# Names moved in an order written out by hand: block 0's row fetch, five pieces of list scatters, two accumulating scatters, one normalisation step

## The chip, the cores and the metric

The kernel runs on one core of a Trainium2 chip. The metric is device time in microseconds of one execution. An engine here is TensorE (PE, with its weight loads as PEld), VectorE (DVE), ScalarE (ACT), GpSimd (POOL) or SyncE (SP), which only issues DMAs. Each engine works through its own instructions in order.

## The reference, cut to what matters

Eight sequences of 512 tokens, 256 wide, go through two layers.

```python
x = x + L0_ffn(L0_cond(x))          # low-rank adapter, then a fake-quantised gated FFN
h = L1_cond(x)                      # per-language adapter, LayerNorm with per-language gamma and beta
probs = softmax(h @ Wr)             # 9 experts, each token goes to its top 2
topk_w, topk_idx = top_k(probs, 2); topk_w = topk_w / sum(topk_w)
x = x + sum over the 2 experts e:  w_e * ((silu(h @ Wg[e]) * (h @ Wu[e])) @ Wd[e])
```

The second layer's experts take 2 x 4096 token rows. Which rows go to which expert is known only on the chip.

## The kernel before, in words

The first part (up to about 85 us) does layer 0 up to its hidden activations. The second part mixes three streams of small steps ("pieces"), each a Python function that issues the instructions of one step for one batch or block:

- for each batch b (0 to 7): the end of layer 0 (qa, qd, dp, dv), the adapter of layer 1 (ap, aa, xp, xa, zp, zv), LayerNorm (np, nv, na, nw), transposes (tp, ta), the router (cp, ce, ct, cv, ca) and ranks (hp, hv);
- hg, for batch b and quarter j: two indirect DMAs on POOL (line 880) that scatter 128 rows of the batch, 1040 bytes each, into the expert lists in DRAM;
- for each block i of 128 list rows (the experts' work): R fetches the rows (four DMAs on line 1057 and a tag on line 1060, issued by SP), U and W fetch the expert's gate/up and down weights (lines 1067 and 1077, 1408 and 768 KB, skipped when the buffer already holds that expert), t transposes the rows on DVE (line 1088), g multiplies by gate and up on TensorE (line 1098), va to vd do SiLU and the product, w the row weights, d multiplies by down (line 1146), y scales the result on DVE (line 1152), and s adds it into the output with an accumulating indirect DMA on POOL (line 1156).

The plan of the first eight blocks is made after two batches, that of the next after six (pp, pw, lines 953 to 1015).

The order of the pieces is the string ORDER (line 58), and `run` (line 1192) issues them one after the other. From it follows each engine's and each queue's order. Nothing is rearranged afterwards, except that waits on semaphores are put in where a piece needs another's result or reuses a buffer. Waits that matter here:

- R reads the lists at places known only on the chip, so it waits for all list scatters that stand before it in ORDER, and a list scatter waits for all R that stand before it;
- s adds into rows known only on the chip, so each s waits for the s before it to have landed, and for the plain writes of the output (xs, line 710) before it;
- y alternates between three buffers (`y_sb[i % 3]`), so y5 waits for s2, y6 for s3, y7 for s4; row and tag buffers go round by eight;
- np, on POOL, computes the power -1/2 of the variance (lines 739 and 740) and needs zv of its batch; nv on DVE needs np.

After block 13 the loop of lines 1230 to 1236 goes on block by block with the same pieces.

Of the kernel before, what the change touches and what calls it, by code (L numbers as in the profile page):

```python
# [55 lines left out]
LAST_LOAD = "L_dT"  # L56
ZEROS_BEHIND = 12
ORDER = """
    qa0d fa1 fa0 fa2 qa0b qd0d qa0a qd0b qa0c fg0 fg1 qd0a qa2b qd0c dp0b qa1b qa1a dp0a qd1b dv0b qd1a dv0a dp1b
    qd2b qa2a xp0_1 dv1b xp0_0 ap0 xa0_1 qd2a xa0_0 dp1a qa2c xs0 aa0 qd2c qa4a zp0_0 dv1a zp0_1 zv0_0 qa3b ap1 fa3  # L60
    zv0_1 qa3a dp2a qd3b np0 aa1 qd3a dp2b dv2a pu1 pd0 nv0 dp3a dv2b na0_1 qd4a pu2 na0_0 nw0_1 xp1_1 ap2 qa4c
    xa1_1 nw0_0 xp1_0 qa4b zp1_1 dv3a xa1_0 tp0_0 pu0 aa2 zv1_1 zp1_0 ta0_0 qd4b tp0_1 qa5b zv1_0 dp3b ta0_1 qd4c
    np1 qa6b cp0 dv3b xs1 dp4b qd5b ce0 qa5a nv1 fa4 ct0 ap3 dv4b na1_1 mz0 cv0 dp4a na1_0 qa6c pd2 xp2_0 aa3 pd1
    xp2_1 nw1_1 hp0 ca0 fg2 xa2_1 hv0 tp1_1 xa2_0 zp2_1 ta1_1 xs2 nw1_0 hg0_0 zp2_0 zv2_1 tp1_0 fa5 ta1_0 zv2_0
    hg0_2 cp1 qd5a ce1 dv4a ct1 fg3 cv1 dp5b hg0_1 ap4 qd6b ca1 hp1 dv5b np2 aa4 dp5a hv1 qa6a hg0_3 nv2 pp0a qa7a
    pw0a dv5a pp0b pw0b na2_1 ap5 hg1_1 qd6a na2_0 pp0c qd6c nw2_1 dp6b qa7b hg1_3 nw2_0 xp3_1 xp3_0 xa3_1 pw0c fg4
    tp2_0 xa3_0 zp3_1 ta2_0 hg1_2 dv6b xs3 tp2_1 zv3_1 zp3_0 ta2_1 U0 qd7b cp2 aa5 zv3_0 hg1_0 ce2 fa6 dp6a qd7a
    ct2 dp7a dv6a np3 cv2 U1 dp7b W1 ap6 nv3 ca2 R0 dv7b na3_1 hp2 dv7a na3_0 xp4_0 hv2 xa4_0 xp4_1 nw3_0 R1 zp4_0
    xa4_1 zp4_1 nw3_1 tp3_0 aa6 t0 tp3_1 ta3_0 zv4_1 g0a W0 ta3_1 xs4 w0 zv4_0 fa7 cp3 va0 t1 hg2_1 g0b ce3 w1 fg5
    ct3 g0c vb0 np4 cv3 U2 g1a vc0 hg2_0 W2 nv4 g1b ca3 U3 vd0 va1 na4_1 hg2_2 g1c vb1 na4_0 nw4_1 d0 vc1 U4 hg2_3  # L70
    nw4_0 vd1 tp4_1 y0 xp5_0 ta4_1 s0 xp5_1 xa5_0 tp4_0 xa5_1 fg6 zp5_0 ta4_0 zp5_1 zv5_0 W3 cp4 zv5_1 ap7 ce4 R2
    ct4 np5 hp3 aa7 cv4 xs5 hv3 ca4 R3 nv5 hp4 hv4 na5_0 na5_1 t2 xp6_1 R4 w2 g2a xa6_1 nw5_0 nw5_1 tp5_0 va2 zp6_1
    ta5_0 t3 R5 d1 w3 zv6_1 t4 w4 tp5_1 y1 R6 xp6_0 ta5_1 s1 g2b xa6_0 zp6_0 vb2 W4 cp5 zv6_0 R7 g2c ce5 np6 g3a t5
    vc2 w5 nv6 vd2 ct5 xs6 na6_0 g3b U5 cv5 na6_1 d2 va3 fg7 hg3_3 nw6_1 ca5 nw6_0 hp5 W5 hg3_1 tp6_1 g3c hv5 ta6_1
    y2 tp6_0 vc3 U6 t6 xp7_0 hg4_0 ta6_0 w6 xp7_1 vb3 xa7_0 xa7_1 vd3 zp7_0 pp1a hg5_3 zv7_0 cp6 g4a ce6 pw1a xs7
    hg4_1 pp1b va4 g4b pw1b pp1c vb4 hg3_0 g4c pw1c d3 t7 vc4 U7 w7 hg3_2 vd4 g5a y3 W6 s2 d4 va5 hg4_3 g5b y4 W7
    s3 g5c vb5 hg4_2 g6a vc5 U8 vd5 hg5_2 g6b va6 g6c vb6 hg5_0 d5 vc6 U9 vd6 hg5_1 zp7_1 y5 ct6 W8 g7a zv7_1 s4
    cv6 d6 np7 va7 R8 nv7 ca6 na7_0 g7b s5 y6 na7_1 nw7_0 R9 hp6 g7c hv6 tp7_0 nw7_1 vc7 s6 ta7_0 R10 t8 tp7_1 w8
    g8a vb7 ta7_1 vd7 t9 d7 va8 w9 U10 R11 g8b y7 t10 s7 w10 cp7 vb8 g8c ce7 R12 ct7 g9a vc8 cv7 g9b va9 W10 t11
    ca7 U11 vd8 g9c w11 vb9 hg6_2 W9 d8 t12 vc9 w12 vd9 U12 hg6_1 g10a y8 W11 g10b s8 va10 hg6_3 g10c vb10 d9 vc10  # L80
    U13 vd10 hg6_0 g11a y9 W12 s9 d10 va11 R13 g11b y10 s10 g11c vb11 R14 g12a vc11 vd11 t13 d11 va12 w13 U14 R15
    g12b t14 y11 s11 g12c vb12 W14 hp7 vc12 R16 g13a hv7 vd12 pp2a va13 g13b pw2a R17 pp2b vb13 d12 pw2b W13 pp2c
    y12 U15 g13c pw2c s12 W15 vc13 hg7_3 U16 vd13 hg7_0 hg7_1 hg7_2
"""
BLOCKS_IN_ORDER = 14

# [1234 lines left out]
```

## Time and profile before

| | us |
|---|---|
| median of 9 runs | 727.85 |
| lowest, highest | 725.87, 733.16 |
| the profiled execution | 733.25 |
| its span on the core | 731.5 |
| TensorE busy in the span | 676.3 (92%) |
| DVE, ACT, POOL busy | 338.4, 202.1, 206.7 |

In the profile's timelines a line gives the start in the span, the duration, the engine, the line of the kernel, what is written and read and how many instructions are merged; in brackets stand the idle time before it and what ended it. SPq is the queue of SP's DMA issues. In the page's slices each digit is the busy share of a fortieth of the span in tenths.

### The profile page before, as it was taken

How to read it: one execution, taken by the hardware profiler on the slowest of the kernel's cores; microseconds unless marked ns; L12 is line 12 of the kernel's file. 1: busy time of each engine (PE TensorE's matmuls, PEld its weight loads, DVE VectorE, ACT ScalarE, POOL GpSimd, SP SyncE). 2: the span in 40 equal slices, each digit the busy share in tenths (PEclk: the TensorE clock that was granted, in tenths of full speed). 3: DMA queues.
4: the chain of work that ended last, by engine and by line, in shares of the span. 5: the costliest groups of instructions: out<-in, count | busy, mean ns of one | idle time of the engine just before them, and what ended most of it. 6: DMA issues, size and time to landing. Idle time of an engine off the chain costs nothing. (4 is left out here: it accounts for less than half of the span.)

```text
span 731.5 us, 14632 instructions
## 1 busy us (share of the span) xinstructions
PE 676.3 (92%) x4678; PEld 569.8 (78%) x4688; DVE 338.4 (46%) x1036; ACT 202.1 (28%) x407; POOL 206.7 (28%) x190
## 2 busy tenths in 40 slices
PE   9989798678786899999999999999999999999995
PEld 3333254337685789898999999999999999999994
DVE  3989778555763164343333333333333333333331
ACT  4698686432422031111111111111111111111110
POOL 1046304605155524343112121212112112211212
PEclk9999898789897989999999999999999999999998
DMA  9500049357467968333356533279924488235742
GB/s 356 196 4 1 1 166 360 119 164 229 84 184 233 307 175 230 60 67 55 56 135 198 160 46 51 45 224 337 290 31 117 101 286 256 32 43 152 231 89 32
DMA packets 86641, 107.91 MB, mean 148 GB/s; under 512 B 58904, under 2 KB 75424, under 8 KB 82976
## 3 DMA queue, kind: packets, MB, share of 16 engines
q1 hardware_dynamic: 73696, 89.61, 39.7%
q0 software_dynamic: 12720, 17.31, 12.4%
q8 instruction: 39, 0.64, 0.3%
q14 instruction: 42, 0.34, 0.2%
q10 hardware_dynamic: 144, 0.01, 0.0%
HBM read 183.55 MB, written 22.83 MB: 282 GB/s over the span
## 5 line engine op out<-in xcount | busy, mean ns | idle before, releaser
L1098 PE MATMUL bank<-upper__104,lower 128*128 128x128 f32 x2636 | 315.8, 278 | 9.6 <-issue 6.4
L1098 PEld LDWEIGHTS bank<-upper__104,lower 128*128 128x128 f32 x2636 | 311.5, 195 | 15.4 <-issue 8.8
L1156 POOL DMA_INDIRECT out_dram<-upper__104,tag x67 | 103.9, 1551 | 370.1 <-DVE upper__104 L1088 277.4
L1114 DVE TENSOR_TENSOR upper__104<-bank,upper__104 128x512 f32<-128x512 f32 x67 | 46.3, 692 | 173.0 <-PE bank L1098 150.1
L1108 ACT ACTIVATE upper__104<-bank 128x512 f32<-128x512 f32 x67 | 40.0, 597 | 245.6 <-PE bank L1098 190.0
L880 POOL DMA_INDIRECT lists<-row,sloti x64 | 63.5, 992 | 49.4 <-issue 18.2
L1146 PE MATMUL bank<-upper__104 128*128 128x256 f32 x312 | 73.5, 386 | 0.0
L1146 PEld LDWEIGHTS bank<-upper__104 128*128 128x128 f32 x312 | 58.8, 195 | 7.3
L1146 PE MATMUL tok<-upper__104 128*128 128x256 f32 x216 | 49.6, 379 | 0.0
L1146 PEld LDWEIGHTS tok<-upper__104 128*128 128x128 f32 x216 | 39.7, 190 | 4.6
L1146 PE MATMUL bank<-lower,upper__104 128*128 128x256 f32 x180 | 41.9, 380 | 1.2 <-issue 1.2
L1124 ACT ACTIVATE upper__104<-bank 128x128 f32<-128x128 f32 x41 | 11.4, 278 | 112.6 <-PE bank L1098 99.5
L1152 DVE TENSOR_SCALAR upper__104<-bank,wt 128x256 f32<-128x256 f32 x41 | 19.8, 484 | 46.7 <-PE bank L1146 42.7
L1098 PE MATMUL tok<-upper__104,lower 128*128 128x128 f32 x312 | 39.1, 275 | 0.0
L1146 PEld LDWEIGHTS bank<-lower,upper__104 128*128 128x128 f32 x180 | 33.0, 190 | 5.9 <-issue 1.9
L1098 PEld LDWEIGHTS tok<-upper__104,lower 128*128 128x128 f32 x312 | 36.9, 192 | 0.0
L1130 DVE TENSOR_TENSOR upper__104<-bank,upper__104 128x128 f32<-128x128 f32 x41 | 11.9, 290 | 41.0 <-ACT upper__104 L1125 34.2
L718 PE MATMUL tok<-w,ha 65*128 65x256 f32 x64 | 19.2, 439 | 12.4 <-ACT xtok L706 8.3
L506 ACT ACTIVATE g<-wide,swg 128x1024 f32<-128x1024 f32 (+1 forms) x24 | 24.1, 1041 | 3.1 <-PE wide L482 2.5
L1124 ACT ACTIVATE upper__104<-tok 128x128 f32<-128x128 f32 x26 | 7.2, 278 | 64.1 <-PE tok L1098 64.1
L718 PEld LDWEIGHTS tok<-w,ha 65*128 65x128 f32 x64 | 12.8, 216 | 15.2 <-ACT xtok L706 8.8
L640 PE MATMUL bank<-yq,wdT 128*128 128x512 bf16 x75 | 21.6, 412 | 1.0 <-DVE yq L628 0.5
(215 smaller groups left out, 699.7 us busy)
## 6 DMA issues: line engine op xcount, KB each, us to landing
lower<-in_L_ffn_W_dram SPq DMA_DIRECT2D x73, 1408.0 KB
upper__104<-in_L_ffn_W_dram SPq DMA_DIRECT2D x48, 768.0 KB
lower<-in_L_ffn_W_dram SPq DMA_DIRECT2D x24, 768.0 KB
lower<-lists SPq DMA_DIRECT2D x144, 32.0 KB
upper__104<-lists SPq DMA_DIRECT2D x140, 32.0 KB
x_sb<-in_x_dram SPq DMA_DIRECT2D x8, 512.0 KB
out_dram<-xtok SPq DMA_DIRECT2D x8, 512.0 KB
lists<-pad SPq DMA_DIRECT2D x10, 130.0 KB
```

The costliest lines, as they stand in the source:

```text
L506: nc.scalar.activation(g, pg, AF.Silu, scale=swg[:, m : m + 1])
L640: nc.tensor.matmul(pd, lhsT=wdT[:, m, cs], rhs=hq_sb[b % 2][:, m], start=m == 0, stop=False)
L718: nc.tensor.matmul(pz[:, j * D : (j + 1) * D], lhsT=ha_sb[b % 2][:, at : at + P], rhs=batches[b]["w2"], start=False, stop=True, skip_group ...
L880: nc.gpsimd.indirect_dma_start(out=own_rows[(b * NJ + j) * 2 + n], out_offset=bass.IndirectOffsetOnAxis(ap=sloti_sb[b % 3][:, j, n : n + 1 ...
L1098: nc.tensor.matmul(pg[:, at * P : (at + 1) * P], lhsT=gu_sb[i % NW][:, c, n * P : (n + 1) * P], rhs=xbT_sb[i % 3][:, c], start=c == 0, sto ...
L1108: nc.scalar.activation(g_sb[i % 3][:, :4].rearrange("p m t -> p (m t)"), held.pop(("pg", i, "a")), AF.Silu)
L1114: nc.vector.tensor_tensor(hid_sb[i % 3][:, :4].rearrange("p m t -> p (m t)"), held.pop(("pg", i, "b")), g_sb[i % 3][:, :4].rearrange("p m ...
L1124: nc.scalar.activation(gs[:, 4], pg[:, :P], AF.Silu)
L1130: nc.vector.tensor_tensor(hid[:, 4], pg[:, P : 2 * P], gs[:, 4], ALU.mult)
L1146: nc.tensor.matmul(po[:, :D], lhsT=hid_sb[i % 3][:, m], rhs=dn_sb[i % NW][:, m], start=m == 0, stop=m == NM - 1)
L1152: nc.vector.tensor_scalar(y_sb[i % 3], held.pop(("po", i))[:, :D], small_["wt"][i % NX], None, ALU.mult)
L1156: nc.gpsimd.indirect_dma_start(out=out, out_offset=bass.IndirectOffsetOnAxis(ap=tag_sb[i % NX][:, 0:1].bitcast(I32), axis=0), in_=y_sb[i % 3],
```

## The change

Only the string ORDER changes; the same 588 names are in it, and it is wrapped at another width, so that all later line numbers are lower by one. In place of the diff, whose every line is rewrapped, here are the moves:

```diff
- cv2 U1 dp7b W1 ap6 nv3 ca2 R0 dv7b
+ cv2 R0 U1 dp7b W1 ap6 nv3 ca2 dv7b

- g5a y3 W6 s2 d4 va5 hg4_3 g5b y4 W7 s3 g5c vb5 hg4_2 g6a vc5 U8 vd5 hg5_2 g6b va6 g6c vb6 hg5_0 d5 vc6 U9 vd6
- hg5_1 zp7_1 y5 ct6 W8 g7a zv7_1 s4 cv6 d6 np7 va7 R8
+ g5a y3 W6 hg4_3 hg4_2 hg5_2 hg5_0 hg5_1 d4 va5 g5b y4 W7 g5c vb5 g6a vc5 U8 vd5 g6b va6 g6c vb6 d5 vc6 U9 vd6
+ zp7_1 s2 y5 ct6 W8 g7a zv7_1 np7 s3 s4 cv6 d6 va7 R8
```

The orders of TensorE, DVE and ACT stay as they were. On SP the five DMAs of R0 now stand ahead of the two of U1 and W1. On POOL five hg (ten list scatters) stand ahead of s2, and np7 ahead of s3 and s4. R0 still stands behind every list scatter of batches 0 and 1. y5 still waits for s2 and y6 for s3; the tag fetches of R10 and R11 now also wait for s2 and s3.

More of the change, by code (lines that the diff above doesn't have):

```diff
@@ L58 @@
 ORDER = """
[L59 to L83, printed above, removed]
+    qa0d fa1 fa0 fa2 qa0b qd0d qa0a qd0b qa0c fg0 fg1 qd0a qa2b qd0c dp0b qa1b qa1a dp0a qd1b dv0b qd1a dv0a dp1b qd2b
@@ new lines @@
+    qa2a xp0_1 dv1b xp0_0 ap0 xa0_1 qd2a xa0_0 dp1a qa2c xs0 aa0 qd2c qa4a zp0_0 dv1a zp0_1 zv0_0 qa3b ap1 fa3 zv0_1
+    qa3a dp2a qd3b np0 aa1 qd3a dp2b dv2a pu1 pd0 nv0 dp3a dv2b na0_1 qd4a pu2 na0_0 nw0_1 xp1_1 ap2 qa4c xa1_1 nw0_0
+    xp1_0 qa4b zp1_1 dv3a xa1_0 tp0_0 pu0 aa2 zv1_1 zp1_0 ta0_0 qd4b tp0_1 qa5b zv1_0 dp3b ta0_1 qd4c np1 qa6b cp0 dv3b
+    xs1 dp4b qd5b ce0 qa5a nv1 fa4 ct0 ap3 dv4b na1_1 mz0 cv0 dp4a na1_0 qa6c pd2 xp2_0 aa3 pd1 xp2_1 nw1_1 hp0 ca0 fg2
+    xa2_1 hv0 tp1_1 xa2_0 zp2_1 ta1_1 xs2 nw1_0 hg0_0 zp2_0 zv2_1 tp1_0 fa5 ta1_0 zv2_0 hg0_2 cp1 qd5a ce1 dv4a ct1 fg3
@@ new lines @@
+    cv1 dp5b hg0_1 ap4 qd6b ca1 hp1 dv5b np2 aa4 dp5a hv1 qa6a hg0_3 nv2 pp0a qa7a pw0a dv5a pp0b pw0b na2_1 ap5 hg1_1
+    qd6a na2_0 pp0c qd6c nw2_1 dp6b qa7b hg1_3 nw2_0 xp3_1 xp3_0 xa3_1 pw0c fg4 tp2_0 xa3_0 zp3_1 ta2_0 hg1_2 dv6b xs3
+    tp2_1 zv3_1 zp3_0 ta2_1 U0 qd7b cp2 aa5 zv3_0 hg1_0 ce2 fa6 dp6a qd7a ct2 dp7a dv6a np3 cv2 R0 U1 dp7b W1 ap6 nv3
+    ca2 dv7b na3_1 hp2 dv7a na3_0 xp4_0 hv2 xa4_0 xp4_1 nw3_0 R1 zp4_0 xa4_1 zp4_1 nw3_1 tp3_0 aa6 t0 tp3_1 ta3_0 zv4_1
+    g0a W0 ta3_1 xs4 w0 zv4_0 fa7 cp3 va0 t1 hg2_1 g0b ce3 w1 fg5 ct3 g0c vb0 np4 cv3 U2 g1a vc0 hg2_0 W2 nv4 g1b ca3
@@ new lines @@
+    U3 vd0 va1 na4_1 hg2_2 g1c vb1 na4_0 nw4_1 d0 vc1 U4 hg2_3 nw4_0 vd1 tp4_1 y0 xp5_0 ta4_1 s0 xp5_1 xa5_0 tp4_0
+    xa5_1 fg6 zp5_0 ta4_0 zp5_1 zv5_0 W3 cp4 zv5_1 ap7 ce4 R2 ct4 np5 hp3 aa7 cv4 xs5 hv3 ca4 R3 nv5 hp4 hv4 na5_0
+    na5_1 t2 xp6_1 R4 w2 g2a xa6_1 nw5_0 nw5_1 tp5_0 va2 zp6_1 ta5_0 t3 R5 d1 w3 zv6_1 t4 w4 tp5_1 y1 R6 xp6_0 ta5_1 s1
+    g2b xa6_0 zp6_0 vb2 W4 cp5 zv6_0 R7 g2c ce5 np6 g3a t5 vc2 w5 nv6 vd2 ct5 xs6 na6_0 g3b U5 cv5 na6_1 d2 va3 fg7
+    hg3_3 nw6_1 ca5 nw6_0 hp5 W5 hg3_1 tp6_1 g3c hv5 ta6_1 y2 tp6_0 vc3 U6 t6 xp7_0 hg4_0 ta6_0 w6 xp7_1 vb3 xa7_0
@@ new lines @@
+    xa7_1 vd3 zp7_0 pp1a hg5_3 zv7_0 cp6 g4a ce6 pw1a xs7 hg4_1 pp1b va4 g4b pw1b pp1c vb4 hg3_0 g4c pw1c d3 t7 vc4 U7
+    w7 hg3_2 vd4 g5a y3 W6 hg4_3 hg4_2 hg5_2 hg5_0 hg5_1 d4 va5 g5b y4 W7 g5c vb5 g6a vc5 U8 vd5 g6b va6 g6c vb6 d5 vc6
+    U9 vd6 zp7_1 s2 y5 ct6 W8 g7a zv7_1 np7 s3 s4 cv6 d6 va7 R8 nv7 ca6 na7_0 g7b s5 y6 na7_1 nw7_0 R9 hp6 g7c hv6
+    tp7_0 nw7_1 vc7 s6 ta7_0 R10 t8 tp7_1 w8 g8a vb7 ta7_1 vd7 t9 d7 va8 w9 U10 R11 g8b y7 t10 s7 w10 cp7 vb8 g8c ce7
+    R12 ct7 g9a vc8 cv7 g9b va9 W10 t11 ca7 U11 vd8 g9c w11 vb9 hg6_2 W9 d8 t12 vc9 w12 vd9 U12 hg6_1 g10a y8 W11 g10b
@@ L84 @@
+    s8 va10 hg6_3 g10c vb10 d9 vc10 U13 vd10 hg6_0 g11a y9 W12 s9 d10 va11 R13 g11b y10 s10 g11c vb11 R14 g12a vc11
+    vd11 t13 d11 va12 w13 U14 R15 g12b t14 y11 s11 g12c vb12 W14 hp7 vc12 R16 g13a hv7 vd12 pp2a va13 g13b pw2a R17
+    pp2b vb13 d12 pw2b W13 pp2c y12 U15 g13c pw2c s12 W15 vc13 hg7_3 U16 vd13 hg7_0 hg7_1 hg7_2
 """
```

## The prediction

> **What bounds the kernel now.** I read the page's 40 slices first, then the table by stage, then TensorE's timeline with the cause of each idle time, then the timelines of the two queues that the change reorders (SP and POOL) and of DVE beside them. The page:
>
> ```profile
> span 731.5 us, 14632 instructions
> PE 676.3 (92%) x4678; PEld 569.8 (78%) x4688; DVE 338.4 (46%) x1036; ACT 202.1 (28%) x407; POOL 206.7 (28%) x190
> ...
> PE   9989798678786899999999999999999999999995
> ...
> DMA  9500049357467968333356533279924488235742
> ```
>
> One slice is 18.3 us. From slice 17 on (about 300 us) PE stands at 9 to the end: the block loop is bound by TensorE, and whatever TensorE is ahead or behind by at 300 us is kept to the end. So each part is worth what it moves in TensorE's arrival there. Both places that the change touches, 150 to 165 us and 230 to 275 us, lie in front of that, where TensorE still waits.
>
> First place: TensorE's, DVE's and SP's timelines, and the table by 2 us, whose last three columns are granted clock, DMA share and GB/s.
>
> ```profile
> 160.35 0.66 PE L776 MATMUL bank<-ident,row 128*128 128x128 f32 x4 [0.63 <-DVE row L768]
> 164.07 3.52 PE L1098 MATMUL bank<-upper__104,lower 128*128 128x128 f32 x16 [3.07 <-DVE upper__104 L1088]
> ...
> 163.71 0.50 DVE L1088 STREAM_TRANSPOSE upper__104<-lower 128x128 f32<-128x128 f32 x2 [3.42 <-DMA lower<-lists]
> ...
> 153.76 0.37 SPq L1067 DMA_DIRECT2D lower<-in_L_ffn_W_dram  x1
> 154.47 0.34 SPq L1077 DMA_DIRECT2D upper__104<-in_L_ffn_W_dram  x1
> 155.89 1.93 SPq L1057 DMA_DIRECT2D lower<-lists  x4
> ...
> 158.00:160.00 2.00, 1.71 (x10) 1.15 (x9) 1.93 (x4) 1.22 (x4) 0.00 (x0) 1.00 0.93 385
> 162.00:164.00 2.00, 0.00 (x0) 0.00 (x0) 0.29 (x2) 0.00 (x0) 0.00 (x0) 1.00 0.10 14
> 164.00:166.00 2.00, 1.93 (x10) 1.93 (x11) 1.87 (x9) 0.00 (x0) 0.00 (x0) 0.60 0.34 76
> ```
>
> Block 0's first matmuls (line 1098) wait 3.07 us for t0 (line 1088), and t0 waits 3.42 us for the rows of R0 (line 1057). R0 was issued behind U1 and W1, 1408 and 768 KB. These do move: the share stands at 0.93 to 0.99 until 162 us. After the gap the clock is at 0.60.
>
> Second place: POOL's and TensorE's timelines.
>
> ```profile
> 232.82 1.60 POOL L1156 DMA_INDIRECT out_dram<-upper__104,tag  x1 [3.95 <-DVE nb L982]
> 240.25 1.60 POOL L1156 DMA_INDIRECT out_dram<-upper__104,tag  x1 [3.27 <-DVE upper__104 L1152]
> 251.03 0.96 POOL L880 DMA_INDIRECT lists<-row,sloti  x1 [0.31 <-issue]
> 252.30 1.60 POOL L1156 DMA_INDIRECT out_dram<-upper__104,tag  x1 [0.30 <-issue]
> 263.00 0.23 POOL L739 TENSOR_SCALAR va<-mv 128x4 f32<-128x4 f32 x1 [9.10 <-DVE lg L815]
> 264.56 1.62 POOL L1156 DMA_INDIRECT out_dram<-upper__104,tag  x1 [0.20 <-issue]
> 269.35 1.59 POOL L1156 DMA_INDIRECT out_dram<-upper__104,tag  x1 [3.17 <-DVE slot L869]
> ...
> 254.27 2.15 PE L1098 MATMUL bank<-upper__104,lower 128*128 128x128 f32 x7 [1.14 <-issue]
> 256.21 4.61 PE L1146 MATMUL bank<-upper__104 128*128 128x256 f32 x12
> 260.66 1.03 PE L718 MATMUL tok<-w,ha 65*128 65x256 f32 x4
> ```
>
> In order these are s2, s3, the last list scatter hg5_1, s4, np7, s5, s6. np7 had POOL free for 9.10 us: it waited for DVE (zv7_1), not for a scatter. TensorE's gaps at 252 to 254 us are "issue": nothing visible held it. In such stretches (173 to 179, 212 to 231, 250 to 254 us) ACT, DVE and SP also take about 0.7 us for a next instruction, and in each of them list scatters (line 880) run together with a weight load.
>
> **Part A: R0 ahead of U1 and W1.** SP's issue before them (the b1c pair) ends at 151.78. U1 came 1.98 us later (two register loads); R0 has one load, and R1's took 0.80 us (158.36 to 159.16), so R0 starts at 152.6. Its five DMAs take 2.47 us as before. They landed for t0 7.8 us after the first issue, behind 2.2 MB; even at that R0 is in at 160.4. DVE is free for t0 at 160.29 (end of line 768), TensorE at 161.01. So the 3.07 us go, wholly. The low clock goes with them: block 0's first 16 matmuls took 3.52 us against 1.95 in the row at 266.02, 1.57 us, and the router's 16 took 0.75 against 0.65. That is 4.7 us at most.
>
> The Trainium skill, "TensorE: Matmul & The Clock Gate", section "What's actually happening", says that the clock halves after at least one idle window of about 3.4 us and comes back after a busy one. The gap here is 3.07 us, and the clock halved all the same; by that rule alone the gap would not lower the clock, and the saving would be 3.1 us, which speaks for less.
>
> What is late next is t1. U1, W1 and R1 start 3.3 us later (R0's 0.80 and 2.47), so the load burst ends at 165.5 instead of 162.2, with R1's rows behind it. R1 no longer waits for U1's and W1's completions before its issue (it lost 2.1 us so), and I put its rows at 167. TensorE could be at g1a at 166.7 (16 matmuls 1.78, 16 of the router 0.6, 16 more 1.78, 12 more 1.33, from 161.1); before it got there at 171.5 (170.21 and 12 of 111 ns). Ends: 4.8 us if the rows are in time, 1.5 us if R1 is 3.3 us later than that. I take 3.8, t1 a microsecond late, as the burst's own length gives it. hg2_1 and np4 on POOL wait for R1 having read the lists, so they start up to 1.5 us later; na4 behind them ran at 179.65, nine microseconds after np4, and hides it. On SP xs4, fa7 and fg5 follow within 0.6 us of before, since xs4 waited for ACT or the loads anyway.
>
> **Part B: five hg pieces ahead of s2 and s3.** Each hg is two scatters on POOL at 1.27 us start to start. Before, the last ten ran from 234.72 to 252, held by s2 (3.95 us, until xs7's rows were in) and by s3 (3.27 us, until y3). Now they follow the others without a break: 229.2 to 241.8. R8, the first read that needs them, was issued at 262.23 behind W8, so their earlier end alone is worth nothing. What may be worth something is the company. U6 was issued at 236.88; eight of the ten then ran beside loads, now four do. If the stretch at 250 goes, the nine matmuls after 251.09 take 1.0 us and d5 2.6 (263.43 to 266.02), so zp7_1 starts at 254.5 instead of 260.66: 6.1 us. Ends: 6.1 gained; or a loss of the size of the 217 us stretch, 8.25 us idle and 3.3 at half clock (2.07, 1.08 and 3.78 against 1.03, 0.65 and 1.95), 11.6. Half the overlap is gone, so I take half of 6.1, 3.0.
>
> Against it stands the Trainium skill, "DMA: Bandwidth & Descriptors", section "Issuing engines are not separate DMA queues": scatters issued by GpSimd and loads issued by SP run on the same 16 DMA engines and interleave. Read strictly, the bytes only change places and B is worth 0; the sum would be 1.9 us.
>
> **Part C: s2, s3 and s4 later, np7 ahead of s3.** np7 gains nothing (its 9.10 us were DVE's). s2 comes at 242, and y5, which reuses its buffer, is at 260.87: hidden by 14 us. R10's tag waits for s2, R11's for s3: both land before those issues (269 to 276). s3 is the matter. It now stands behind np7, so it starts where s5 did, 1.65 us after zv7_1's end (262.91). y6 writes the buffer that s3 reads and must wait until s3 has landed. A scatter takes about 4.1 us from its start to its completion (the trace's completion events; 264.56 to 269.35 is 4.79 from one to the next that waits for it). So y6 moves from 3.3 to 5.7 us after zv7_1; behind it on DVE are nw7_0, hv6 and nw7_1, and TensorE's tp7_1 waits for nw7_1: it goes from 8.23 to 10.15 us after zv7_1. Cost 1.9 us, below 3.4 of idle. Ends: 0 if DVE's order leaves slack, 5 if s3 lands as late as s4 did at 252.30 (6.5 us) and the clock falls. s4 to s7 follow 4.8 us apart, s7 at 283.7 instead of 276.94; hg6 and s8 come 1.7 us later, and R13, at 298.79, still finds the lists written. After that the chain has caught up.
>
> **Sum.** 3.8 + 3.0 - 1.9 = 4.9 us. The profiled execution took 733.25 us, 1.75 around its span of 731.5; that is 5.4 above the median of 727.85, among the slowest three of nine (730.83 to 733.16). Profiled, after would be 728.4. From the median, 723.0, 0.67% less.
>
> **The rivals.** (1) The forecast: A and half of B, 723.0; by itself 718.5 to 724.2. For it: a named wait that ends on the critical engine. (2) B is worth nothing, because the stretch at 250 us is one that the median run does not have (the profiled run is 5 us slower than the median, about one such stretch), or because the bytes only move: 3.8 - 1.9 = 1.9, 726.0, within 0.5%. Against: the two other stretches are too long to be all missing from the median run. (3) Slower: the uncut scatter burst extends the stretch that now ends at 231 us. Place: 231 to 243 us, on all engines, while U6 and W5 load. At the pace of 252 to 254 us (two matmuls in 2.1 us) it takes about 10 of these 12 us, and half clock behind it 3 more: 13 - 6.1 - 3.8 + 1.9 = 5.0, 732.9. It decides from a stretch of 11.7 us on. For it: the 217 us stretch grew under 14 such scatters without a break. Against: between 232 and 236 us the DMA share is low (0.04 at 232). (4) The np7 move does nothing by itself: already in the sum.
>
> **How the numbers follow.** Forecast 0.48, (2) 0.30, (3) and a part A lost to R1 0.22. About 0.5% (3.6 us) is what a measurement of this kernel can tell from no change: faster below 724.2, slower above 731.5. The low end is A without t1's wait and all of B: 4.8 + 6.1 - 1.9 = 9.0, rounded to 718.5; the high end is where the slower cases begin, with 2 in 10 beyond.
>
> **What would show it.** A: t0 at 160.3 with no wait for the lists, g0a at about 161 in 2 us, clock 1.0 until 168; wrong if t1 waits past 168. B: ten list scatters between 229 and 242 (earlier by A's gain), no issue gaps around 251; wrong if gaps stand at 235 to 243. C: y6 ended by an out_dram DMA, tp7_1 some 2 us idle. The forecast is wrong if TensorE's 300 us mark is not ahead.

## The result, and the profile after

The changed kernel takes 741.24 us (median of 20 runs, 732.51 to 744.58); the kernel before, beside it, 727.81 us (62 runs, 722.73 to 740.46). The ratio, taken over the runs in the chip's faster state alone, is 1.0158, 95% interval 1.0134 to 1.0182, which is 11.5 us, while the medians over all runs are 13.4 us apart. So it is 1.6% slower, where 0.7% faster was forecast. The profiled execution took 741.35 us with a span of 739.6, so it stands for the median, whereas the profiled execution of before (733.25 us) lay 5.4 us above its own.

The page of the changed kernel, answering the slices of before:

```profile
span 739.6 us, 14631 instructions
...
PE   9989798698783989998999999999999999999995
...
PEclk9999899798796999998999999999999999999998
DMA  8500059457384776333356633269933489225742
```

A slice is 18.5 us. PE's ninth digit (148 to 166 us, part A's place) has risen from 7 to 9, its thirteenth (222 to 240 us, part B's) has fallen from 6 to 3, and the clock's stands at 6 there.

Part A's place, TensorE's timeline of the changed kernel:

```profile
158.73 0.66 PE L775 MATMUL bank<-ident,row 128*128 128x128 f32 x4 [0.67 <-DVE row L767]
159.22 1.95 PE L1097 MATMUL bank<-upper__104,lower 128*128 128x128 f32 x16
...
163.67 6.42 PE L1097 MATMUL bank<-upper__104,lower 128*128 128x128 f32 x56
...
177.54 2.94 PE L717 MATMUL tok<-w,ha 65*128 65x256 f32 x7 [2.71 <-ACT xtok L705]
```

g0a, the first multiplications of block 0 (the row at 159.22), starts with no wait and takes 1.95 us, as forecast, and g1a follows unbroken. At 177.5 us there is a wait that before did not have there.

Part B's place. First POOL:

```profile
215.80 0.96 POOL L879 DMA_INDIRECT lists<-row,sloti  x1 [3.02 <-DVE upper__104 L1151]
217.06 0.96 POOL L879 DMA_INDIRECT lists<-row,sloti  x1 [0.30 <-issue]
...
237.33 0.96 POOL L879 DMA_INDIRECT lists<-row,sloti  x1 [0.30 <-issue]
238.59 1.61 POOL L1155 DMA_INDIRECT out_dram<-upper__104,tag  x1 [0.30 <-issue]
262.75 0.23 POOL L738 TENSOR_SCALAR va<-mv 128x4 f32<-128x4 f32 x1 [22.54 <-DVE lg L814]
264.30 1.64 POOL L1155 DMA_INDIRECT out_dram<-upper__104,tag  x1 [0.20 <-issue]
268.77 1.56 POOL L1155 DMA_INDIRECT out_dram<-upper__104,tag  x1 [2.83 <-DMA out_dram<-upper__104,tag]
```

Eighteen list scatters stand 1.27 us apart from 215.80 to 238.3 without a break, then s2, np7, s3, s4. TensorE beside them, and SP's queue:

```profile
220.47 1.77 PE L1097 MATMUL bank<-upper__104,lower 128*128 128x128 f32 x13
222.95 0.50 PE L1097 MATMUL bank<-upper__104,lower 128*128 128x128 f32 x3 [0.71 <-issue]
233.40 0.63 PE L962 MATMUL bank<-after,onesf 9*128 9x32 f32 x2 [9.95 <-DVE cum L988]
...
238.58 1.14 PE L1145 MATMUL bank<-lower,upper__104 128*128 128x256 f32 x2 [0.22 <-issue]
241.37 0.38 PE L1145 MATMUL bank<-lower,upper__104 128*128 128x256 f32 x1 [1.66 <-issue]
242.07 2.73 PE L1145 MATMUL bank<-lower,upper__104 128*128 128x256 f32 x6 [0.33 <-issue]
...
249.78 8.20 PE L1097 MATMUL bank<-upper__104,lower 128*128 128x128 f32 x72
```

```profile
216.97 0.40 SPq L709 DMA_DIRECT2D out_dram<-xtok  x1
243.08 0.33 SPq L1066 DMA_DIRECT2D lower<-in_L_ffn_W_dram  x1
```

The gaps of 250 to 254 us are gone (72 matmuls in 8.20 us), as part B meant. In their place TensorE stands or crawls from 223 to 243 us (the 9.95 us are a wait for DVE, which itself stood still), and SP issues nothing for 26 us. The table by 4 us of the same kernel says what runs meanwhile (its columns: PE, weight loads, DVE, ACT, POOL, granted clock, DMA share, GB/s):

```profile
220.00:224.00 4.00, 2.74 (x22) 2.38 (x20) 0.00 (x0) 0.27 (x1) 3.08 (x4) 1.00 0.96 350
224.00:228.00 4.00, 0.00 (x0) 0.00 (x0) 0.00 (x0) 0.00 (x0) 3.08 (x4) 0.72 0.78 281
228.00:232.00 4.00, 0.00 (x0) 0.00 (x0) 0.00 (x0) 0.60 (x1) 3.04 (x4) 0.50 0.30 109
232.00:236.00 4.00, 2.60 (x12) 2.42 (x13) 0.73 (x4) 0.00 (x0) 2.88 (x3) 0.50 0.29 100
236.00:240.00 4.00, 3.38 (x11) 2.15 (x10) 0.00 (x0) 0.00 (x0) 3.33 (x3) 0.57 0.28 100
```

From 228 us on the bytes are the scatters' own: 128 rows of 1040 bytes in 1.27 us are 105 GB/s, and the table shows 100 to 109. No weight load is under way, and still, up to 232 us, hardly anything but POOL works; from 233 to 237 us TensorE runs twelve matmuls unbroken at half clock, then the gaps come back.

Part C's place, and what comes of it later:

```profile
270.55 0.63 PE L775 MATMUL bank<-ident,row 128*128 128x128 f32 x4 [1.14 <-DVE place L860]
273.04 0.63 PE L775 MATMUL bank<-ident,row 128*128 128x128 f32 x4 [1.86 <-DVE row L767]
273.51 3.56 PE L1097 MATMUL bank<-upper__104,lower 128*128 128x128 f32 x16
...
329.44 2.75 PE L1145 MATMUL bank<-upper__104 128*128 128x256 f32 x12
332.04 3.56 PE L1097 MATMUL bank<-upper__104,lower 128*128 128x128 f32 x28
335.82 0.27 PE L1097 MATMUL bank<-upper__104,lower 128*128 128x128 f32 x1 [0.22 <-issue]
336.54 0.60 PE L1097 MATMUL bank<-upper__104,lower 128*128 128x128 f32 x3 [0.45 <-issue]
337.95 0.59 PE L1097 MATMUL tok<-upper__104,lower 128*128 128x128 f32 x3 [0.82 <-issue]
339.38 2.08 PE L1097 MATMUL tok<-upper__104,lower 128*128 128x128 f32 x9 [0.84 <-issue]
341.26 4.73 PE L1145 MATMUL tok<-upper__104 128*128 128x256 f32 x12
345.82 4.40 PE L1097 MATMUL bank<-upper__104,lower 128*128 128x128 f32 x38
```

```profile
268.60 0.48 DVE L1151 TENSOR_SCALAR upper__104<-bank,wt 128x256 f32<-128x256 f32 x1 [2.86 <-DMA out_dram<-upper__104,tag]
```

y6 (the DVE line) waits 2.86 us for s3. Before tp7_0 and tp7_1 TensorE is idle 3.00 us, against 1.03 us ahead of tp7_1 before; the granted clock is 0.62 and then 0.50 until 277 us, and g8a takes 3.56 us instead of 1.95. At 335 us, at the end of batch 7's eight list scatters (326.4 to 336 us), issue gaps come back, longer than in the kernel before, whose two gaps there end at 333.2 us. From 330 to 334 us, ahead of these gaps, the DMA share is 0.27 to 0.28 at 100 GB/s, the scatters' own pace, so here slowing starts with no weight load beside it.

For the comparisons below I use one distance in TensorE's timeline: from the start of xp7_0 (the last `tok<-ident,x_sb` row ahead of zp7_0) to the start of zp7_1 (the next `tok<-w,ha` row after zp7_0). It spans all of block 4 to 6's work beside these scatters: 216.42 to 260.66 = 44.24 us in the profile of before, 215.02 to 260.40 = 45.38 after. Where nothing slows it, it is 26.95, as some runs below show. The two differ by 1.1 us only, but the profiled execution of before lay 5.4 us above its median, and A alone, with the scatters as before, has 41.50 and 39.35 below; a pair of traces nearer to their medians comes at the end of the experiments.

### The profile page after: what moved, and what is told of

The parts are those of the page before. It is cut to its first block, busy times and chain, and to the rows that moved or that the text cites. A ratio compares the mean times of both kernels' runs of the same rounds, so it can differ in the third digit from the quotient of the medians.

```text
span 739.6 us, 14631 instructions
## 1 busy us (share of the span) xinstructions
PE 679.2 (92%) x4678; PEld 571.4 (77%) x4688; DVE 338.1 (46%) x1036; ACT 202.0 (27%) x407; POOL 207.8 (28%) x190
## 3 DMA queue, kind: packets, MB, share of 16 engines
q0 software_dynamic: 12720, 17.31, 12.5%
## 5 line engine op out<-in xcount | busy, mean ns | idle before, releaser
L1145 PE MATMUL bank<-upper__104 128*128 128x256 f32 x312 | 71.7, 379 | 0.0
L1145 PE MATMUL tok<-upper__104 128*128 128x256 f32 x216 | 51.6, 390 | 0.0
L1145 PE MATMUL bank<-lower,upper__104 128*128 128x256 f32 x180 | 44.4, 393 | 2.8 <-issue 2.2
L1145 PEld LDWEIGHTS tok<-upper__104 128*128 128x128 f32 x216 | 41.2, 197 | 5.2
L505 ACT ACTIVATE g<-wide,swg 128x1024 f32<-128x1024 f32 (+1 forms) x24 | 24.1, 1040 | 3.1 <-PE wide L481 2.5
L1151 DVE TENSOR_SCALAR upper__104<-tok,wt 128x256 f32<-128x256 f32 x26 | 12.6, 484 | 23.3 <-PE tok L1145 23.3
L1129 DVE TENSOR_TENSOR upper__104<-tok,upper__104 128x128 f32<-128x128 f32 x26 | 7.6, 292 | 32.0 <-ACT upper__104 L1124 32.0
```

Of the source, the lines that this page charges most:

```text
L505: nc.scalar.activation(g, pg, AF.Silu, scale=swg[:, m : m + 1])
L1129: nc.vector.tensor_tensor(hid[:, 4], pg[:, P : 2 * P], gs[:, 4], ALU.mult)
L1145: nc.tensor.matmul(po[:, :D], lhsT=hid_sb[i % 3][:, m], rhs=dn_sb[i % NW][:, m], start=m == 0, stop=m == NM - 1)
L1151: nc.vector.tensor_scalar(y_sb[i % 3], held.pop(("po", i))[:, :D], small_["wt"][i % NX], None, ALU.mult)
```

## The experiments

The theory after the result: what costs the time is list scatters that follow each other on POOL at full pace; while they do, the other engines take about 0.7 us, or a multiple of it, for a next instruction. s2 and s3, waiting in the middle of them, had broken their run. Rivals: the loss is part C's waits; or the moved fetch itself; or only the number or place of the scatters counts. The runs came from several chips; each group has its own runs of before beside it on the same chip, and ratios are to those.

### The three parts alone

```diff
- cv2 U1 dp7b W1 ap6 nv3 ca2 R0 dv7b
+ cv2 R0 U1 dp7b W1 ap6 nv3 ca2 dv7b
```

> Only R0 is moved ahead of U1 and W1; scatters, np7 and s2 to s4 stay as before. Theory (the loss comes from the unbroken run of list scatters, part A is a gain): TensorE passes 170 us about 3.6 us earlier and keeps it, 724 us (722 to 726). Rival (the moved fetch is itself the loss, through a later t1 or because every later scatter now starts 3.6 us earlier beside other loads): 728 us or more.

728.31 us beside 729.01, ratio 0.998 (0.994 to 1.002).

```diff
- W6 s2 d4 va5 hg4_3 g5b y4 W7 s3 ... hg4_2 ... hg5_2 ... hg5_0 ... hg5_1
+ W6 hg4_3 hg4_2 hg5_2 hg5_0 hg5_1 s2 d4 va5 g5b y4 W7 s3 ...
```

> Only the five hg pieces are moved: they stand ahead of s2, s2 and s3 directly behind them, so neither breaks the run of list scatters any more; s4 and np7 as before. Theory (a long unbroken run of list scatters slows every engine to about 0.7 us an instruction): one stretch reaches to about 243 us, 733 to 738 us. Rival (the loss is that s3 and s4 stand behind np7): 728 us, no change.

737.60 us (four runs), ratio 1.013 (1.005 to 1.020); xp7_0 to zp7_1 takes 45.59 us.

```diff
- y4 W7 s3 g5c ... zv7_1 s4 cv6 d6 np7 va7 R8
+ y4 W7 g5c ... zv7_1 np7 s3 s4 cv6 d6 va7 R8
```

> Only np7 is moved ahead and s3 behind it; s2 still breaks the run of list scatters, s3 no longer does (the run behind s2 is ten scatters without a break). Theory: y6 waits for s3's landing and TensorE loses 1.9 us and 1.6 us of low clock, 3.5 us, 731 us (729 to 735, the upper end if the ten scatters without a break also stretch). Rival (this move is the main loss): 738 us or more.

732.96 us, ratio 1.007 (1.003 to 1.011); xp7_0 to zp7_1 takes 38.79 us. TensorE's timeline there shows the same wait and low clock as the changed kernel:

```profile
262.85 0.63 PE L776 MATMUL bank<-ident,row 128*128 128x128 f32 x4 [0.97 <-DVE place L861]
265.34 0.80 PE L776 MATMUL bank<-ident,row 128*128 128x128 f32 x4 [1.86 <-DVE row L768]
265.93 3.45 PE L1098 MATMUL bank<-upper__104,lower 128*128 128x128 f32 x16
```

So by the ratios, on 729.01 us, A is -1.4 us (-4.5 to 1.7), B +9.3 (3.6 to 14.8), C +5.0 (2.0 to 8.0). They add up to 12.9, against 11.5 (1.58% of 727.81) for the whole change: B and C account for it. B is the larger by the ratios, but its interval does not tell it from C. A alone met its rival, not the theory.

### Pacing the scatters of the changed kernel

```diff
 def hg(b, k):
     for n in range(2):
+        if b >= 3:
+            for _ in range(2):
+                nc.gpsimd.tensor_scalar(idle_sb, one_sb, 1.0, None, ALU.add)   # 128x4, read by nobody
         nc.gpsimd.indirect_dma_start(...)
```

> The changed kernel, with two small POOL operations of 0.23 us (on four columns of a tile that nothing reads) ahead of every list scatter of batches 3 to 7, so that scatters start some 1.9 us apart rather than 1.27; nothing is left out of the computation. Theory (pace of the scatters, each engine's dispatch is starved while they come back to back): the stretch from 223 to 243 us goes or shrinks, 728 to 734 us. Rival (what counts is how many scatters there are, or their place beside something else): the stretch stays or grows with the run, 741 us or more.

732.87 us, ratio 1.007 (1.002 to 1.011), 0.9% less than the changed kernel's. In this and the other paced kernels line numbers are up to 6 higher. POOL's timeline, then TensorE's and DVE's:

```profile
223.37 1.04 POOL L886 DMA_INDIRECT lists<-row,sloti  x1 [0.16 <-issue]
224.44 0.54 POOL L885 TENSOR_SCALAR idle_sb<-one_sb 128x4 f32<-128x4 f32 x2
225.15 1.04 POOL L886 DMA_INDIRECT lists<-row,sloti  x1 [0.16 <-issue]
```

```profile
223.38 2.75 PE L1152 MATMUL bank<-upper__107 128*128 128x256 f32 x12
225.97 4.29 PE L1104 MATMUL bank<-upper__107,lower 128*128 128x128 f32 x37
...
256.02 0.21 PE L851 MATMUL bank<-both,upper 128*128 128x36 bf16 x1 [12.12 <-DVE both L833]
```

```profile
252.06 0.48 DVE L1158 TENSOR_SCALAR upper__107<-bank,wt 128x256 f32<-128x256 f32 x1 [16.57 <-DMA out_dram<-upper__107,tag]
```

With 0.54 us of other POOL work ahead of each scatter (1.78 us apart) the stretch is gone: xp7_0 to zp7_1 takes 26.95 us instead of 45.38, the same scatters, bytes and order. POOL is as busy as before, so it is not POOL's being busy, but scatters at full pace. The rival "number or place" falls for this stretch. At zp7_1 TensorE is 24 us ahead of the profile of before (236.60 against 260.66), and loses most of it again: s2 now stands behind all paced scatters, at 247.91, and y5 waits 16.57 us for it. The second half of the change, moving s2 behind, was harmless only while TensorE was late.

### Pacing with s2 and s3 in place

Here A (R0 ahead) is kept, but hg, s2, s3, s4 and np7 stand as before.

> The kernel before with R0 moved ahead and with two small POOL operations ahead of every list scatter of batches 3 to 7; s2, s3, np7 and s4 stay where they were before. With the scatters paced and y5 not held by a late s2, theory (pace) says: no stretch between 205 and 250 us, y5 some 13 us earlier than in the paused changed kernel, and the end of the scatters (about 251 us, for R8 and np7) sets the pace there: 708 to 720 us. Rival (the time at 300 us is set by R8's rows or np7 anyway, and the stretches only hide that wait): 724 to 729 us.

734.53 us, ratio 1.008 (1.004 to 1.012); neither theory had it. xp7_0 to zp7_1 takes 26.95 us, so there is no stretch, but the scatters now end at 258.1, np7 behind them runs at 260.08, and TensorE's tp7_0 waits 16.59 us.

> As the paused kernel with s2 to s4 in place, with one small POOL operation instead of two ahead of each list scatter: some 1.5 us apart. Theory (pace): if 1.5 us is wide enough, the scatters end 6 us earlier and the time is 2 to 6 us below that of two operations; if it is not, a stretch comes back and the time is 5 to 12 us above it. Rival (number of scatters): as with two.

One operation (1.49 us apart): 720.75 us beside 727.86, ratio 0.991 (0.987 to 0.994), 13.8 us less than with two, where 2 to 6 were expected; xp7_0 to zp7_1 is 31.89 us, of which some 5 are a short stretch at 217 to 222 us. The scatters end at 243.4, and np7 waits for DVE, not they for it. This is faster than both kernels of the case.

> The same pauses as with s2 to s4 in place, but R0 at its place of before, so the difference of the two is part A without the stretches' scatter in the times. Part A worth its wait and low clock: 3 to 4 us above the kernel with R0 ahead. Rival (A is hidden by what comes at 250 to 270 us, R8 and np7, once the stretches are gone): within 1 us of it.

Two operations, R0 at its place of before: 735.89 us, ratio 1.008 (1.003 to 1.014), 1.4 us above the same with R0 ahead, inside both intervals: no sign of 3.6 us. In its trace TensorE waits 3.12 us for t0, and is held by np7 all the same (16.35 us ahead of tp7_0).

```diff
+        if n == 0 and f"{b}{k}" in ("40", "41", "32", "42", "50", "62", "60", "73", "71"):
+            for _ in range(8): nc.gpsimd.tensor_scalar(idle_sb, one_sb, 1.0, None, ALU.add)
```

> The changed kernel with its run of list scatters cut into fours by eight small POOL operations (about 2.1 us) each time; the mean pace is that of the kernel with two operations ahead of every scatter, but inside a four the scatters follow at 1.27 us. Theory as first told (the unbroken run has to be long): the stretch goes as with even pauses, 729 to 735 us. Rival (every scatter at 1.27 us behind another slows the engines, however short the run): part of the stretch stays, 736 to 742 us.

731.97 us, ratio 1.007 (1.003 to 1.011), as with even pauses (732.87). Fours at 1.27 us with 2.4 us of rest between them: 30.29 us from xp7_0 to zp7_1, with one wait of 2.16 us and no stretch. Short runs at full pace do no visible harm; the mean pace here is also that of the even pauses, so run length and mean pace are not told apart.

### What is left of the change once paced, and part A

> The changed kernel with one small POOL operation ahead of every list scatter of batches 3 to 7 (1.5 us apart). Theory: the stretch that cost the changed kernel its lead is gone; what is left of the change's cost beside the paused kernel with s2 to s4 in place (720.75 us) is y5's wait for s2, which comes behind the scatters (some 4 us), and y6's for s3 (1.9 to 3.5 us): 725 to 729 us. Rival (the moves cost nothing but the stretch): 720 to 722 us.

726.20 us beside 728.94, ratio 0.994 (0.990 to 0.997): with one small operation ahead of each scatter the changed kernel is no longer slower than before. In its trace y6 waits 5.23 us for s3 and g8a runs at half clock (3.62 us); y5's wait, which I had expected, is not there. Issue gaps come back at 238 to 242 us, at the end of the unbroken row.

> The kernel before with one small POOL operation ahead of every list scatter of batches 3 to 7, R0 at its place of before; beside 720.75 us with R0 ahead the difference is part A. Theory (A is 3.6 us in every run): 723.5 to 725 us. Rival (the lead of A is eaten by a later wait): 720 to 722 us.

722.04 us beside 728.94, ratio 0.990 (0.985 to 0.995): the same as with R0 ahead (0.991). Its profiled execution took 718.21. Here too the rival has it: part A adds nothing.

> R0 ahead, s2 to s4 in place, one small POOL operation ahead of the list scatters of batches 3 to 5 alone, none ahead of those of 6 and 7. Theory: the first gain is kept, 719 to 721 us; if the eight scatters of batch 7 without a break bring a stretch at about 320 us (4.8 us of it in the changed kernel), up to 725 us.

723.02 us, ratio 0.990 (0.985 to 0.994): pausing batches 6 and 7 as well is worth nothing that the medians tell apart, although this trace has the gaps under batch 7's scatters (321 to 324 us) that the expectation named.

> R0 ahead, s2 to s4 in place, one small POOL operation ahead of the first scatter of each pair alone, so 1.27 us and 1.5 us in turn. Theory as refined by the runs so far (a POOL instruction between the scatters is what ends the slowing, since fours at 1.27 us left no stretch): as with one ahead of each, 718 to 722 us. Rival (the mean pace counts, and 1.4 us is too dense): a stretch comes back, 724 to 728 us.

724.48 us, ratio 0.992 (0.988 to 0.995), at the low edge of the rival's 724 to 728. Its profiled execution (728.92, 4.4 above the median) has stretches at 221 to 229 and 249 to 253 us, xp7_0 to zp7_1 42.57 us; so at 1.4 us apart on average they can come back, although a POOL operation stands between every second scatter and the next; the rival had it so. The intervals do not tell it from one pause for each.

### R0 ahead or not, all scatters paced

Four kernels in two pairs: one operation ahead of every list scatter, or four ahead of every second pair; with R0 ahead, or not.

> R0 ahead, s2 to s4 in place, one small POOL operation ahead of every list scatter of all batches, so also of batch 2's eight at 160 to 175 us, where the traces with R0 ahead show ScalarE and TensorE idle 5 us to about 177 us. Theory (part A's lead runs into the slowing of batch 2's scatters and is lost there): 716 to 719 us, 1.5 to 3.5 us below the same pauses without R0 ahead. Rival (A is worth nothing because t0's wait was short anyway, 0.2 to 1.1 us in three of five traces without the move): as without R0 ahead, within 1 us.

> The kernel before, one small POOL operation ahead of every list scatter of all batches. Theory (the early scatters at 125 to 145 us and 160 to 175 us slow the engines too): 717 to 721 us, below the 722.0 us of pauses from batch 3 on. Rival (those early scatters are too few in a row to matter): 722 us or, by their later end, more.

> R0 ahead, s2 to s4 in place, and all list scatters cut into fours by four small POOL operations (about 1.1 us) ahead of every third pair, with 1.27 us inside a four: the same number of POOL operations as one ahead of each. Theory that the length of the unbroken run counts, and four is short enough: no stretch left, 714 to 718 us. Rival that the mean pace counts: as with one ahead of each scatter, within 2 us of it.

> The kernel before with all list scatters cut into fours in the same way, R0 at its place of before: beside the last one it is part A once more. A lost to t0's short wait: the same time within 1 us; A worth its 3.6 us: 3 to 4 us more.

717.01, 716.63, 716.96 and 716.49 us, ratios 1.006, 1.007, 1.006 and 1.006 (each within 0.0025). They ran on a chip on which the kernel before takes 712.02 us (21 runs, 710.23 to 715.91), 16 us less than on the others. All four traces have 26.95 us from xp7_0 to zp7_1 and no issue gaps over 0.5 us from 130 to 275 us. There the pauses cost 0.6%, and in the traces np7 stands behind the slower scatters; an unpaced trace of that chip does not exist. POOL's and DVE's timelines with one pause each and R0 ahead:

```profile
246.46 1.62 POOL L1162 DMA_INDIRECT out_dram<-upper__107,tag  x1 [0.30 <-issue]
248.15 0.21 POOL L742 TENSOR_SCALAR va<-mv 128x4 f32<-128x4 f32 x1
248.44 1.04 POOL L743 TENSOR_TENSOR r<-va,half 128x4 f32<-128x4 f32 x1
```

```profile
249.52 0.16 DVE L749 SCALAR_TENSOR_TENSOR q<-r 128x4 f32<-128x4 f32 x1 [13.45 <-POOL r L743]
```

As for part A, the lead is there at first: the `both,upper` row that waits for DVE comes at 179.25 and 178.95 us with R0 ahead, at 180.87 and 181.01 without, 1.6 and 2.1 us. It is lost in this wait for np7. The question of run length against mean pace got no answer, since none of these traces shows any slowing.

### The two once more

> R0 ahead alone, unpaused, once more. On a chip where the kernel before takes about 712 us: part A's lead of 2.7 us (the trace of the paused pair there) is kept if nothing behind it waits for the end of the scatters, 709 to 710 us; hidden by np7 or R8, 712 us. On a chip where before takes about 728 us: theory (the lead runs into the slowing behind it) 0 to 2 us below before; rival (A is 3.6 us) 724 to 725 us.

> The changed kernel once more, beside another run of before. On a chip where before takes about 712 us: theory (the loss is the slowed dispatch, which is absent there, and y5's and y6's waits for s2 and s3, which are not) no stretch of issue gaps between 220 and 245 us, 0 to 5 us above before, 712 to 717 us; rival (the change loses through waits alone) 722 us or more. On a chip where before takes about 728 us: stretch there, 738 to 742 us.

On another chip, before 727.40 us: R0 ahead alone 727.73, ratio 1.001 (0.997 to 1.005); the changed kernel 740.25, ratio 1.016 (1.010 to 1.022), xp7_0 to zp7_1 44.44 us, with the stretch from 221 to 242 us. Its part C lines are those of the first: y6 waits 2.62 us, g8a takes 3.29. These two traces, of one chip, 12.5 us apart in their spans as in their medians, split the loss of B and C: the changed kernel is 0.7 us behind at xp7_0 (214.01 against 213.30), 5.8 at zp7_1 (258.45 against 252.65), 9.4 at 281 us (the row of 44 matmuls behind g8, 281.34 against 271.97) and 12.7 at block 14's first row (342.21 against 329.49). So 5.1 us come from the stretch, 3.6 from part C's place and 3.4 from under batch 7's scatters. Neither of the two ran on the chip of 712 us, so what the change does there stays open.

The same distance over the unpaced and paced kernels, each from one profiled execution, with the ratio of its medians (not of that execution):

| list scatters of batches 3 to 5 | xp7_0 to zp7_1, us | ratio |
|---|---|---|
| unbroken ten behind the others: the change, again, B alone | 45.38, 44.44, 45.59 | 1.016, 1.016, 1.013 |
| as before; A alone, again; C alone (s2's wait kept, s3's gone) | 44.24; 41.50, 39.35; 38.79 | 1; 0.998, 1.001; 1.007 |
| one pause a pair | 42.57 | 0.992 |
| one pause each (changed; A; A, batches 3 to 5 alone; before) | 35.04; 31.89; 32.84; 31.94 | 0.994; 0.991; 0.990; 0.990 |
| eight pauses a four, changed | 30.29 | 1.007 |
| two pauses each (changed; A; before) | 26.95; 26.95; 26.95 | 1.007; 1.008; 1.008 |

## Why the prediction was wrong

**The base** held: the profiled execution of before is some 5 us above the median, and the after one is not, so forecasting from the median was right. Two slips in its sums change nothing: 251.09 + 1.0 + 2.6 is 254.7, not 254.5, and 727.85 - 9.0 is 718.85, not 718.5.

**Part B failed, in the step "What may be worth something is the company".** It took the slowed stretches to need list scatters together with a weight load, counted eight overlapped scatters before and four after, and took a gain of half of 6.1 us. The table of the changed kernel shows 12 us of slowing with no load under way, under batch 7 the gaps also start without one, and the paced kernel shows full speed (TensorE busy without a gap from 216 to 240 us) with loads and scatters side by side, the DMA share at 0.96 to 1.06. What the stretches need is scatters back to back; the two waits that the change took out of their run, 3.95 and 3.27 us of POOL standing idle at s2 and s3, had broken it. Of these s2's was enough: C alone keeps it (3.60 us at 228 us there) and leaves out s3's, and its distance of 38.79 us is no longer than that of A alone. Measured: +9.3 us for B alone (3.6 to 14.8), 5.1 in the pair of traces, in place of -3.0. Its bound upward, 11.6, held for these values, not for the whole interval. Rival (3) had this mechanism and the place (a stretch drawn out to 243 us); its sum, 732.9, lies 8 us too low: it had 3.8 us of gain for A (1.4 measured), a net loss of 6.9 for B (9.3) and 1.9 for C (5.0). Its "against", the low DMA share at 232 us, was no argument, since the DMA share is low in the stretch itself (0.28 to 0.30). The weight of 0.22 on it was the misjudgement. The Trainium skill, "DMA: Bandwidth & Descriptors", section "Issuing engines are not separate DMA queues", by which B would be worth 0 because the bytes only change places, is not contradicted on the bytes, but the time differs by 9.3 us here. With the DMA engines at 0.28 to 0.30 from 228 us on, it is not their bandwidth that runs out.

**Part A failed, in the step "So the 3.07 us go, wholly".** The step itself came true in the trace: no wait, 1.95 us at full clock, hg2 and R1 as told. But TensorE's wait for t0 in one execution was taken for that of all. In the other six traces without the move it is 0.66, 0.21, 3.12, 1.12, 0.61 and not there at all: 0.95 us on average, where the prediction subtracted the 5.4 us between profiled run and median from the total and from none of its terms. What is left of the lead runs into the next hold: on the chips with stretches a wait of 2 to 5 us for ACT or without visible cause at 174 to 178 us, beside batch 2's eight scatters, in nine of eleven traces with R0 ahead (2.71 in the changed kernel), where the traces without the move have issue gaps; on the other chip np7. Measured: -1.4 and +0.7 us alone, nothing in three paced pairs. That it is batch 2's scatters which hold it there is argued from their place, not shown: the pairs meant to show it ran on the chip of 712 us.

**Part C was right in mechanism and too small, in the term "Cost 1.9 us, below 3.4 of idle".** y6 waits for s3's landing, ended by an out_dram DMA, as told; TensorE's idle time grows by 2.0 us against 1.9 forecast. The clock falls besides, which stood only in the range: 1.6 us. And a third term was missing: from d12's start to block 14's first row TensorE takes 16.38, 16.12 and 15.01 us in the three kernels with part C unpaced (the change, C alone, the change again) and 11.57, 12.23, 12.11 and 11.64 in before, B alone and A alone, twice: some 4 us under batch 7's eight scatters. In the three the scatters start 2.8 to 3.4 us ahead of d12, in the four 4.1. But A with pauses in batches 3 to 5 alone, which has no part C, starts them 3.4 us ahead and takes 14.92 us. So the term goes with scatters that start late, not with part C as such; why they start late, and whether that is what prolongs the gaps, stays open. Measured: +5.0 us alone (2.0 to 8.0), at the upper one of the ends 0 and 5. On the clock: behind 1.14 and 1.86 us of idle time with 0.63 us of matmuls between them the granted clock was 0.62 and then 0.50, behind the gap of 3.07 us before it was 0.60, and behind 1.03 us alone it stayed at 1.00. But with one pause each (R0 ahead, the rest in place) the same pattern, 1.04 and 1.86 us, left it at 1.00:

```profile
253.15 0.63 PE L779 MATMUL bank<-ident,row 128*128 128x128 f32 x4 [1.04 <-DVE place L864]
255.63 0.63 PE L779 MATMUL bank<-ident,row 128*128 128x128 f32 x4 [1.86 <-DVE row L771]
256.10 1.95 PE L1104 MATMUL bank<-upper__107,lower 128*128 128x128 f32 x16
```

So the idle time alone does not decide it, and the 1.6 us are not a fixed price of this wait. The Trainium skill, "TensorE: Matmul & The Clock Gate", section "What's actually happening", names an idle window of about 3.4 us; by it neither the gap of 3.07 us nor the two shorter ones would have lowered the clock.

Together: forecast -3.8 - 3.0 + 1.9 = -4.9; measured part by part -1.4 + 9.3 + 5.0 = +12.9, and +11.5 for the whole. The sign came from B; C was twice its forecast and more.

## What to carry to other kernels

A wait inside a long row of GpSimd scatters may be worth more than it costs: before closing it up, look whether all engines' issue gaps grow with the length of the row, and if so pace it (one 0.23 us operation ahead of each scatter gave 0.9 to 1.0% on the chips where before takes 728 us, and cost 0.6 to 0.7% on the one where it takes 712). Check a wait in a second execution before booking it, since a single trace 5 us above the median contains waits that the median run does not have. When pacing or moving makes one engine earlier, follow what stands behind the paced row on its queue (here s2 for y5, np7 for na7): it becomes the next bound.

## What the runs showed of the hardware that was not expected

While indirect scatters of 128 rows of 1040 bytes follow each other 1.27 us apart on GpSimd, after six to ten of them (six at 222 us and eight at 335 us in the changed kernel, ten at 242 us with C alone) the other engines get gaps between instructions, on TensorE in steps of about 0.7 us (335.82, 336.54, 337.95 and 339.38 us above). TensorE, VectorE and ScalarE stand for up to 9.95, 13.56 and 12.38 us in the changed kernel, in part waiting for one another, also with the DMA engines at 0.28 to 0.30 and no other transfer under way. With 1.78 us from one to the next this does not happen (26.95 us against 45.38 for the same work); with 1.49 us a stretch of about 5 us is left. Through what the engines are held is open, and so is whether the run's length or its mean pace counts. It seems a matter of the chip, too: on one of the chips used the kernel before takes 712 us instead of 728, and with one pause for each scatter the distance is 26.95 us there, against 31.89 to 35.04 on the others (the early batches were paced there as well).
